# Turning the attention weights and the spread of scores by DMA instead of on TensorE

## The chip, the cores and the metric

The kernel runs on one core of a Trainium2 chip. Its engines work side by side, each through a queue of its own in order: TensorE (PE: matmuls and transposes, whose results go to PSUM banks), VectorE (DVE), ScalarE (ACT), GpSimd (POOL), and SyncE (SP), which only issues DMA transfers here. They wait for each other by semaphores. The metric is the device time of one execution, in microseconds (us); less is better.

## The reference, cut to what matters

There are 128 graphs of 128 nodes with 256 features in f32, and an adjacency of 0 and 1 for each graph (one in eight entries set). Two residual layers follow each other:

```python
# layer 0: a gated graph network, 3 steps with shared GRU weights
h = relu(layernorm(x))
for i in range(3):
    m    = h @ weight[i]
    aggr = A^T @ m                       # A = (adj != 0), for each graph
    h    = gru_cell(aggr, h, w_ih, w_hh, b_ih, b_hh)
x = x + h
# layer 1: graph attention
h  = relu(layernorm(x))
Wh = h @ W
s  = Wh.sum(-1)                          # one score for each node
e  = leaky_relu(s[:, :, None] + s[:, None, :], 0.2)
e  = where(adj == 0, -inf, e)
x  = x + softmax(e, -1) @ Wh
```

Two things in layer 1 concern the change. The score of the *second* node, s[q], has to stand along the free dimension of every partition p (the spread of scores). And the weights e[p, q] are needed with q on the partitions when they are multiplied with h, so they have to be transposed (128 x 128 for each graph).

## The kernel before, in words

**Tiling.** The graphs are worked in 32 groups of G = 4. "rows" tiles have nodes on partitions, 4 graphs x 256 features; "hT" tiles have features on partitions, two halves k of 4 x 128 nodes. All working tiles stay on chip; only x, the adjacency and the output move to and from HBM.

**One group.** `group` loads x and adj, normalises (`normed`), and goes through the three GRU steps. Each step sums over edges (`edge_sums`, line 596: f32 state split into three bf16 parts so that the product with a 0/1 matrix is exact) and multiplies state and edge sums with composed weights in `products`. That is one level of a seven-product (Strassen-Winograd) scheme for blocks of two by two: partial sums x, y and q stand in six PSUM banks with one buffer each (`x_rz`, `y_rz`, `q_rz`, and the same with `_n`), matmuls go on accumulating into y after ACT has copied a stage of it out (line 691, tiles `t_rz` and `t_n`; line 701 copies x into y), and DVE adds q to the copies (line 694). After y_rz come the matmuls of y_n, then the next product on y_rz, which needs the copy of y_rz done. Steps 0 and 1 end in `gru`, step 2 in `gru_rows`, which leaves the new x in the tile x1.

**State between layouts.** Where the state changes between rows and hT (groups 3 and on), `turned_halves` does it without PE: ACT copies the f32 data as two planes of 16-bit halves (line 535), SP issues a DMA transpose of them (line 545), ACT puts the halves together again (line 539), once for each k.

**Attention.** `attention(g, ...)` works on x1: `normed` into h1; s by a multiply with the summed weights w1_sum and an accumulated sum (line 867); the mask as 0 or -BIG into e (line 885); the spread of s by four PE transposes of a broadcast column into a "misc" bank (line 891); on DVE the add of that bank (897), the add of s[p] (898), leaky ReLU (900), row maximum (902) and its negation (904); exponentials on ACT (909, with a table load); row sums and reciprocals (911, 912); four PE transposes of e into a "misc" bank (917) and an ACT copy into eT (919); `weighted` multiplies h1 by eT (610) and ACT evicts uT (615); the product with W (930); the update of x1 (935) and the store (938). The last group's attention runs in two halves of two graphs. h1 and eT have one buffer, e, s, uT two, "misc" has two banks.

**The order.** Nothing is issued in the order in which the code calls it. Every piece of work goes into `Plan` by `op(engine, cost in ns, function, reads, writes, ...)`, and `Plan.run` simulates the five queues from these costs: on each engine it takes what can start first, and among those the one with the lowest rank. The rank is the due time less the planned cost of what still depends on the piece, with `MARGIN` taken off ahead of the fixed chain of product matmuls. The product matmuls keep a fixed order of 96 turns (group, step) of SLOT = 18150 planner ns each. The exponentials have to follow a marked copy of turn (g + 2, 1) and then go ahead of everything on ACT. `two=True` marks an operation that holds the SBUF port that DVE and POOL share, `LAG` is the planned time between engines, 4000 for SP (line 545 asks for 4500). The order so found is what the hardware queues get.

The attention of a group is due at the end of the turn of its last step plus three slots:

```python
plan.due = (phase(g, L - 1) + 3) * SLOT
gru_rows(L - 1, hT, hs, aT, gs, rows, x1)
for lo, hi in ((0, G),) if g < NG - 1 else ((G // 2, G), (0, G // 2)):
    attention(g, a, x1, h1, lo, hi)
```

Of the kernel before, what the change touches and what calls it, by code (L numbers as in the profile page):

```python
# [9 lines left out]
BF16 = mybir.dt.bfloat16  # L10
I32 = mybir.dt.int32
U16 = mybir.dt.uint16
AF = mybir.ActivationFunctionType
OP = mybir.AluOpType
AX = mybir.AxisListType

P = 128
G = 4
# [2 lines left out]
SETS = 4  # L21
EARLY = 3
SLOT = 18150
MARGIN = 5000
GATES = 18150
BIG = 3.0e38

# [9 lines left out]
class Plan:  # L37
# [14 lines left out]
    def buf(self, tag):  # L52
        n, kind = self.tags[tag]
        if kind == "free" or kind == "turn":
            b = Buf(tag, tag, None)
            if kind == "turn":
                self.waiting.setdefault(tag, []).append((self.phase, len(self.waiting.get(tag, ())), b))
            return b
        key = (tag, self.group % SETS if kind == "set" else 0)
        uses = self.last.setdefault(key, [])  # L60
        b = Buf(tag, key, uses[-n] if len(uses) >= n else None)
        b.slot = (key[1], len(uses) % n)
        uses.append(b)
        return b
# [146 lines left out]
def kernel(  # L211
# [21 lines left out]
    nc = tc.nc  # L233
    B, N, D = x.shape
    L = weight.shape[0]
    KD = D // P
    NG = B // G
# [5 lines left out]
    work = ctx.enter_context(tc.tile_pool(name="work", bufs=1))  # L243
# [5 lines left out]
        "at": (1, "all", work, [P, G, N]), "a": (6, "all", work, [P, G, N]),  # L249
        "hT": (1, "set", work, [P, KD, GN]), "rows": (3, "turn", work, [P, G, D]),  # L250
        "pl": (1, "turn", work, [P, 2, 3, GN]), "plT": (1, "turn", work, [P, 2, 3, GN]),
        "r1": (1, "turn", work, [P, G, D]), "p3": (1, "turn", work, [P, G, D]),
        "hs": (2, "turn", work, [P, 4, H]), "aT": (2, "turn", work, [P, KD, GN]),
        "gs": (2, "turn", work, [P, 4, H]),
# [21 lines left out]
        "w1": (1, "all", const, [P, KD, D]), "w1_out": (1, "all", const, [P, KD]),  # L276
        "w1_sum": (1, "all", const, [P, D]),
    }
    DTYPE = {"at": I32, "a": BF16, "pl": U16, "plT": U16, "p3": BF16}
    phys = {}  # L280

    def make(tag, n, kind, pool, shape):
# [7 lines left out]
    def ap(b):  # L290
        return phys[(b.tag,) + b.slot]

    plan = Plan({t: v[:2] for t, v in BUFS.items()})
    op, buf = plan.op, plan.buf
# [179 lines left out]
    def normed(src, dst, lo=0, hi=G):  # L474

        st, mv, rs, nm = buf("st"), buf("mv"), buf("rs"), buf("nm")
        part = slice(lo, hi)
        for b in range(lo, hi):
            op("DVE", 415, lambda b=b: nc.vector.bn_stats(ap(st)[:, b, :], ap(src)[:, b, :]),
               [(src, b, b + 1)], [(st, b, b + 1)])  # L480

        def aggr():
            for b in range(lo, hi):
                nc.vector.bn_aggr(ap(mv)[:, b, :], ap(st)[:, b, :])
        op("DVE", 160 * (hi - lo), aggr, [st], [mv])

        def rstd():
            nc.gpsimd.tensor_tensor(ap(rs)[:, part], ap(mv)[:, part, 1], eps[:, part], OP.add)
            nc.gpsimd.tensor_tensor(ap(rs)[:, part], ap(rs)[:, part], neghalf[:, part], OP.pow)
        op("POOL", 1300, rstd, [mv], [rs])  # L490
        op("DVE", 170, lambda: nc.vector.scalar_tensor_tensor(
            ap(nm)[:, part], ap(mv)[:, part, 0], -1.0, ap(rs)[:, part], op0=OP.mult, op1=OP.mult),
           [mv, rs], [nm])
        for b in range(lo, hi):
            op("ACT", 600, lambda b=b: nc.scalar.activation(
                ap(dst)[:, b, :], ap(src)[:, b, :], AF.Relu, bias=ap(nm)[:, b:b + 1],
                scale=ap(rs)[:, b:b + 1]), [(src, b, b + 1), rs, nm], [(dst, b, b + 1)])

    def flat(b):
        return ap(b).rearrange("p q n -> p (q n)")  # L500
# [26 lines left out]
    def turned_halves(src, rows, dst):  # L527

        pl, plT = buf("pl"), buf("plT")

        def planes(b, k):
            return ap(b)[:, k, 0:2].rearrange("p two (g m) -> p two g m", g=G)
        for k in range(KD):
            units = [src] if rows else [(src, 2 * k, 2 * k + 2)]
            op("ACT", 960, lambda k=k: nc.scalar.copy(
                planes(pl, k), halves_of(src, rows)[:, k]), units, [(pl, k, k + 1)])
            transpose(pl, plT, k, 2)
            units = [(dst, 2 * k, 2 * k + 2)] if rows else [dst]
            op("ACT", 960, lambda k=k: nc.scalar.copy(  # L539
                halves_of(dst, not rows)[:, k], planes(plT, k)),  # L540
               [(plT, k, k + 1)], units)

# [272 lines left out]
    def phase(g, layer):  # L815
        return turns.index((g, layer))

    def group(g):
        graphs = slice(g * G, (g + 1) * G)
        plan.phase = phase(g, 0)  # L820
        plan.due = (plan.phase - 1) * SLOT
        rows0, at, a, hT = buf("rows"), buf("at"), buf("a"), buf("hT")
        op("SP", 100, lambda: nc.sync.dma_start(ap(rows0), x[graphs].rearrange("b n d -> n b d")),
           [], [rows0])
        op("SP", 100, lambda: nc.sync.dma_start(ap(at), adj[graphs].rearrange("b n m -> n b m")),
           [], [at])
        op("DVE", 420, lambda: nc.vector.tensor_scalar(ap(a), ap(at), 0.0, None,
                                                       op0=OP.not_equal), [at], [a])
        plan.due = (phase(g, L - 1) + 2) * SLOT
        normed(rows0, rows0)  # L830
        for layer in range(L):
            plan.phase = phase(g, layer)
            if layer == 0:
                if g < EARLY:
                    rows_to_T(rows0, hT)
                else:
                    turned_halves(rows0, True, hT)
                parts = parts_of(rows0)
            elif layer < L - 1:
                parts = turned_parts(hT)  # L840
            else:
                rows, x1, h1 = buf("rows"), buf("x1"), buf("h1")
                turned_halves(hT, False, rows)
                parts = parts_of(rows)
                op("SP", 100, lambda: nc.sync.dma_start(
                    ap(x1), x[graphs].rearrange("b n d -> n b d")), [], [x1])
            hs, aT, gs = buf("hs"), buf("aT"), buf("gs")
            node_sums(hT, hs, "POOL", 1390, 940)
            edge_sums(parts, a, aT)
            node_sums(aT, gs, "DVE", 690, 440)  # L850
            plan.cursor = plan.phase * SLOT
            if layer < L - 1:
                gru(layer, hT, hs, aT, gs)
        plan.due = (phase(g, L - 1) + 3) * SLOT
        gru_rows(L - 1, hT, hs, aT, gs, rows, x1)
        for lo, hi in ((0, G),) if g < NG - 1 else ((G // 2, G), (0, G // 2)):
            attention(g, a, x1, h1, lo, hi)

    def attention(g, a, x1, h1, lo, hi):
# [19 lines left out]
        def es():  # L879
            return ap(e)[:, part]  # L880

        def small(t):
# [1 line left out]
        cost = 155 + 134 * n  # L884
        op("DVE", 150 + 66 * n, lambda: nc.vector.tensor_scalar(
            es(), ap(a)[:, part], 0.0, -BIG, op0=OP.is_equal, op1=OP.mult), [(a, lo, hi)], [e])
        s_all = buf("misc")

        def turn_s():
            for b in range(lo, hi):  # L890
                nc.tensor.transpose(flat(s_all)[:, b * N:(b + 1) * N],
                                    ap(s)[:, b:b + 1].to_broadcast([P, P]), ident)

        def spread():
            return flat(s_all)[:, lo * N:hi * N].rearrange("p (b n) -> p b n", n=N)
        op("PE", 110 * n, turn_s, [s], [s_all], [e])
        op("DVE", cost, lambda: nc.vector.tensor_tensor(es(), es(), spread(), OP.add), [s_all], [e])
        op("DVE", cost, lambda: nc.vector.tensor_tensor(es(), es(), wide(s), OP.add), [s], [e],
           two=True)
        op("DVE", cost, lambda: nc.vector.scalar_tensor_tensor(  # L900
# [6 lines left out]
        def exps():  # L907
            for b in range(lo, hi):
                nc.scalar.activation(ap(e)[:, b, :], ap(e)[:, b, :], AF.Exp, bias=ap(low)[:, b:b + 1])
        op("ACT", 2600 + 390 * n, exps, [low], [e], turn=(g + 2, 1, "rz"))  # L910
        op("DVE", cost, lambda: nc.vector.tensor_reduce(small(den), es(), AX.X, OP.add), [e], [den])
        op("DVE", 170, lambda: nc.vector.reciprocal(small(rden), small(den)), [den], [rden])
        p_e, eT, uT = buf("misc"), buf("eT"), buf("uT")

        def turn():
            for b in range(lo, hi):
                nc.tensor.transpose(flat(p_e)[:, b * N:(b + 1) * N], ap(e)[:, b, :], ident)
        op("PE", 110 * n, turn, [e], [p_e], [eT])
        op("ACT", 190 + 100 * n, lambda: nc.scalar.copy(
            ap(eT)[:, part].rearrange("p b n -> p (b n)"), flat(p_e)[:, lo * N:hi * N]),  # L920
           [p_e], [(eT, lo, hi)])

        weighted(h1, eT, uT, lo, hi)
        for m in range(lo, hi, 2):
# [13 lines left out]
        op("SP", 100, lambda: nc.sync.dma_start(  # L938
            out[g * G + lo:g * G + hi].rearrange("b n d -> n b d"), ap(x1)[:, part]),
           [(x1, lo, hi)], [])  # L940

    weights()
    for g in range(NG):
# [33 lines left out]
```

## Time and profile before

| | |
|---|---|
| median of 3 runs | 2150.49 us (2149.06 to 2151.18) |
| span of the profiled run | 2151.8 us |
| granted TensorE clock, mean | 0.994 |
| ACT copies of line 535, line 539 | 122 of 1046 and 1043 ns; 122 of 1338 ns |
| transposes on PE in the attention | 128 at line 891, 128 at line 917 |
| DMA queue of SP | 24.5% of 16 engines' span |

The page gives, in this order: busy time of each engine with its share of the span and its number of instructions; the same in tenths over 40 equal slices; the DMA queues; the chain of work that ended last, followed back from the last instruction; the costliest groups of instructions, each with its line, engine, operation, tiles written and read, count, busy time, mean time of one, and the idle time of its engine just before it with what ended it. PE is TensorE's matmul row and PEld its weight loads. The ends of matmul records are modelled and overlap with the next, so that the distance from start to start says what a matmul costs.

### The profile page before, as it was taken

Reading aid. Unit: us, or ns where it says so; the run is one execution under the profiler, and the core shown is the slowest. Engines: PE = TensorE matmul, PEld = TensorE weight load, DVE = VectorE, ACT = ScalarE, POOL = GpSimd, SP = SyncE. Lnnn points to the kernel's source line nnn. Section 1 sums busy time; section 2 is a strip of 40 time slices with the busy share of each in tenths; the row PEclk is TensorE's granted clock in tenths of the full one; section 3 lists DMA queues with packets and bytes.
Section 4 is the critical chain, followed back from the end, with each engine's and each line's share of the span. In section 5 each row is a group of like instructions: output and inputs, shape, how many; then the busy total and the mean of one; then the engine's idle time right before and its main releaser. Section 6 shows DMA issues by size and latency. Waiting matters only on the chain.

```text
span 2151.8 us, 34116 instructions
## 1 busy us (share of the span) xinstructions
PE 2124.3 (99%) x12670; PEld 1894.7 (88%) x12670; DVE 1693.9 (79%) x3297; ACT 1543.7 (72%) x2675; POOL 948.4 (44%) x889
## 2 busy tenths in 40 slices
PE   8999999999999999999999999999999999999997
PEld 7888888998889998888998899998899988898885
DVE  5778887887877778777787877878777787877776
ACT  5567877776777777767777777777777778676673
POOL 5645453344544435443445534445534345334331
PEclk9999999999999999999999999999999999999998
DMA  4222122222322222212122223223222213212110
GB/s 142 45 50 50 43 43 64 59 50 50 70 62 57 60 50 50 69 50 69 42 52 65 67 52 62 48 53 66 62 57 60 50 45 69 74 36 49 40 50 30
DMA packets 301750, 121.49 MB, mean 56 GB/s; under 512 B 232976, under 2 KB 301328, under 8 KB 301584
## 3 DMA queue, kind: packets, MB, share of 16 engines
q1 hardware_dynamic: 301584, 119.31, 24.5%
q8 instruction: 99, 1.62, 0.3%
q14 instruction: 67, 0.55, 0.1%
HBM read 45.36 MB, written 16.78 MB: 29 GB/s over the span
## 4 chain that ended last, share of the span: by engine, by line
PE 92%; DVE 5%; DMA 1%; ACT 1%; issue 1%; POOL 0%; DVEq 0%; ACTq 0%; POOLq 0%
PE y_rz L654 14%; PE q_rz L654 10%; PE x_rz L654 10%; PE y_rz L661 8%; PE y_n L654 7%; PE misc L596 6%; PE q_rz L661 5%; PE x_rz L661 5%; PE x_n L654 5%; PE q_n L654 5%; PE misc L930 5%; PE y_n L661 4%; PE x_n L661 3%; PE misc L610 3%; PE q_n L661 3%
## 5 line engine op out<-in xcount | busy, mean ns | idle before, releaser
L624 POOL TENSOR_TENSOR hs<-hT 128x512 f32<-128x512 f32 x96 | 128.8, 1342 | 326.3 <-PE y_n L661 275.9
L556 POOL TENSOR_TENSOR r<-rows 128x512 f32<-128x512 f32 x128 | 146.5, 1163 | 259.8 <-ACT rows L539 170.9
L691 ACT COPY t_rz<-y_rz 128x512 f32<-128x512 f32 x192 | 112.0, 583 | 191.9 <-PE y_rz L654 111.1
L654 PE MATMUL y_rz<-hs,s_hh 128*128 128x256 f32 x768 | 198.6, 381 | 0.2 <-ACT t_rz L691 0.2
L654 PE MATMUL y_rz<-gs,s_x 128*128 128x256 f32 x768 | 197.4, 380 | 0.0
L694 DVE TENSOR_TENSOR t_rz<-t_rz,q_rz 128x512 f32<-128x512 f32 x192 | 131.1, 683 | 70.0 <-ACT t_rz L691 36.5
L654 PEld LDWEIGHTS y_rz<-gs,s_x 128*128 128x128 f32 x768 | 146.4, 191 | 20.0
L654 PEld LDWEIGHTS y_rz<-hs,s_hh 128*128 128x128 f32 x768 | 144.3, 191 | 21.2 <-ACT t_rz L691 1.8
L628 POOL TENSOR_TENSOR hs<-hT,hs 128x256 f32<-128x256 f32 x96 | 75.0, 789 | 196.2 <-PE q_n L661 186.1
L559 POOL TENSOR_TENSOR p<-r 128x512 bf16<-128x512 f32 x128 | 155.5, 1233 | 0.3
L798 POOL TENSOR_TENSOR x<-x,u 128x512 f32<-128x512 f32 x64 | 84.8, 1341 | 157.9 <-DMA x<-in_x_dram 83.6
L691 ACT COPY t_n<-y_n 128x512 f32<-128x512 f32 x192 | 112.4, 585 | 52.3 <-PE y_n L654 20.7
L694 DVE TENSOR_TENSOR t_n<-t_n,q_n 128x512 f32<-128x512 f32 x192 | 131.1, 683 | 23.8 <-ACT t_n L691 9.1
L599 ACT COPY aT<-misc 128x512 f32<-128x512 f32 x192 | 111.7, 584 | 38.0 <-PE misc L596 30.3
L654 PE MATMUL x_rz<-aT,s_x 128*128 128x256 f32 x512 | 131.5, 379 | 0.0
L654 PE MATMUL x_rz<-hT,s_hh 128*128 128x256 f32 x512 | 131.5, 379 | 0.0
L576 POOL TENSOR_TENSOR d<-hT,pl 128x512 f32<-128x512 f32 x64 | 84.1, 1318 | 93.9 <-ACT pl L574 84.1
L930 PE MATMUL misc<-w,uT 128*128 128x256 f32 x512 | 122.8, 384 | 0.3 <-ACT uT L615 0.2
L755 ACT ACTIVATE u<-u,bias_i 128x512 f32<-128x512 f32 x128 | 92.1, 721 | 37.8 <-DVE u L746 37.5
L654 PE MATMUL y_n<-hs,s_hh 128*128 128x256 f32 x384 | 114.5, 380 | 0.3 <-ACT t_n L691 0.2
L654 PE MATMUL y_n<-gs,s_x 128*128 128x256 f32 x384 | 114.3, 379 | 0.0
L763 DVE TENSOR_TENSOR hT<-u,d 128x512 f32<-128x512 f32 x128 | 110.1, 862 | 3.5
(212 smaller groups left out, 6425.7 us busy)
## 6 DMA issues: line engine op xcount, KB each, us to landing
rows<-in_x_dram SPq DMA_DIRECT2D x32, 512.0 KB, 4.3
x<-in_x_dram SPq DMA_DIRECT2D x32, 512.0 KB, 3.9
out_dram<-x SPq DMA_DIRECT2D x31, 512.0 KB, 2.9
at<-in_adj_dram SPq DMA_DIRECT2D x32, 256.0 KB, 2.9
plT<-pl SPq DMA_TRANSPOSE x186, 3.3
rz<-in_L_gnn_w_ih_dram SPq DMA_DIRECT2D x1, 768.0 KB, 5.0
e<-in_L_gnn_weight_dram SPq DMA_DIRECT2D x3, 256.0 KB, 5.6
rz<-in_L_gnn_w_hh_dram SPq DMA_DIRECT2D x1, 768.0 KB, 7.9
```

The source lines that it names most:

```text
L556: op("POOL", 1106, lambda part=part: nc.gpsimd.tensor_tensor(ap(r1)[:, part], ap(rows)[:, part], top(rows)[:, part], OP.subtract), [(rows, ...
L559: op("POOL", 1050, lambda part=part: nc.gpsimd.tensor_tensor(ap(p3)[:, part], ap(r1)[:, part], top(r1)[:, part], OP.subtract), [(r1, n, n ...
L596: nc.tensor.matmul(flat(ps)[:, b * N:(b + 1) * N], part(i, b, k), ap(a)[:, b, :], start=(i == 0), stop=(i == 2))
L599: op("ACT", 590, lambda k=k, ps=ps: nc.scalar.copy(ap(dst)[:, k, :], flat(ps)), [ps], [(dst, 2 * k, 2 * k + 2)])
L624: op(eng, cost, lambda: sub(ap(w)[:, 0:2, :], blocks()[:, 1::2, :], blocks()[:, 0:2, :], OP.subtract), [t], [(w, 0, 2)], two=True)
L654: nc.tensor.matmul(ap(bank)[:, half, :], ap(w)[:, i - 1, q, :], source(t, sums), start=(first and c == 0 and m == 0), stop=False, skip_gro ...
L661: nc.tensor.matmul(ap(bank)[:, m, half * P:(half + len(chunk)) * P], source(t, sums)[:, m * N:(m + 1) * N], ap(w)[:, i - 1, q:q + len(chun ...
L691: op("ACT", 590, lambda: nc.scalar.copy(ap(t), ap(y)), [y], [t])
L694: op("DVE", 690, lambda: nc.vector.tensor_tensor(ap(t), ap(t), ap(q), OP.add), [q], [t])
L755: op("ACT", 723, lambda j=j, cols=cols: nc.scalar.activation(ap(u)[:, cols], ap(u)[:, cols], AF.Tanh, bias=ap(W["bias_i"])[:, 2 * KD + j:2 ...
L763: op("DVE", 690, lambda j=j, d=d, cols=cols: nc.vector.tensor_tensor(ap(hT)[:, j, :], ap(u)[:, cols], ap(d), OP.add), [(u, lo, hi), d], [( ...
L930: nc.tensor.matmul(ap(ps)[:, b, :], ap(uT)[:, k, (m + b) * N:(m + b + 1) * N], ap(w1)[:, k, :], start=(k == 0), stop=(k == KD - 1))
```

## The change

For groups 0 to 29 both transposes of the attention leave PE. A new helper, `turned_halves_of`, does what `turned_halves` does for the state: ACT copies 16-bit halves of the source into "pe" (two planes of 4 x 128), SP issues one DMA transpose into "peT", ACT puts the halves together in the destination. It is used twice for each group: from s, read with stride 0 as a broadcast, into a new tile s_all in SBUF, and from e into eT. The eviction at line 919 and two uses of the "misc" banks go with it. The last two groups keep the transposes on PE. pe, peT and s_all have one buffer each.

It is meant to take transposes off the engine that multiplies. Along with it, planner numbers change: MARGIN, the costs of Relu, of the halves' copies and of the exponentials are set to other values, and the attention of the last two groups gets the same due time, 96.5 slots (97 and 98 before).

```diff
-MARGIN = 5000
+MARGIN = 6000
...
+        "pe": (1, "all", work, [P, 2, G, N]), "peT": (1, "all", work, [P, 2, G, N]),
+        "s_all": (1, "all", work, [P, G, N]),
...
     def normed(src, dst, lo=0, hi=G):
-            op("ACT", 600, lambda b=b: nc.scalar.activation(
+            op("ACT", 520, lambda b=b: nc.scalar.activation(
...
     def turned_halves(src, rows, dst):
-            op("ACT", 960, lambda k=k: nc.scalar.copy(
+            op("ACT", 1045, lambda k=k: nc.scalar.copy(
                 planes(pl, k), halves_of(src, rows)[:, k]), units, [(pl, k, k + 1)])
             transpose(pl, plT, k, 2)
-            op("ACT", 960, lambda k=k: nc.scalar.copy(
+            op("ACT", 1340, lambda k=k: nc.scalar.copy(
...
-        plan.due = (phase(g, L - 1) + 3) * SLOT
+        plan.due = min(phase(g, L - 1) + 3, len(turns) + 0.5) * SLOT
...
-        s_all = buf("misc")
-        op("PE", 110 * n, turn_s, [s], [s_all], [e])
-        op("DVE", cost, lambda: nc.vector.tensor_tensor(es(), es(), spread(), OP.add), [s_all], [e])
+        if g < NG - 2:
+            s_all = buf("s_all")
+
+            def spread():
+                return ap(s_all)
+            turned_halves_of(lambda: ap(s).bitcast(U16).rearrange("p (g two) -> p two g", two=2)
+                             [:, :, :, None].to_broadcast([P, 2, G, N]), s, s_all)
+        else:
+            s_all = buf("misc")
...
+        op("DVE", cost, lambda: nc.vector.tensor_tensor(es(), es(), spread(), OP.add), [s_all], [e],
+           two=g < NG - 2)
...
-        op("ACT", 2600 + 390 * n, exps, [low], [e], turn=(g + 2, 1, "rz"))
+        op("ACT", 2570 * (g < NG - 1) + 320 * n, exps, [low], [e], turn=(g + 2, 1, "rz"))
...
-        p_e, eT, uT = buf("misc"), buf("eT"), buf("uT")
-        op("PE", 110 * n, turn, [e], [p_e], [eT])
-        op("ACT", 190 + 100 * n, lambda: nc.scalar.copy(
-            ap(eT)[:, part].rearrange("p b n -> p (b n)"), flat(p_e)[:, lo * N:hi * N]),
-           [p_e], [(eT, lo, hi)])
+        eT, uT = buf("eT"), buf("uT")
+        if g < NG - 2:
+            turned_halves_of(lambda: halves_of_weights(e), e, eT)
+        else:
+            p_e = buf("misc")
...
+    def halves_of_weights(t):
+        return ap(t).bitcast(U16).rearrange("p g (m two) -> p two g m", two=2)
+
+    def turned_halves_of(halves, src, dst):
+
+        pe, peT = buf("pe"), buf("peT")
+        op("ACT", 1045, lambda: nc.scalar.copy(ap(pe), halves()), [src], [pe])
+        op("SP", 100, lambda: nc.sync.dma_start_transpose(
+            ap(peT).rearrange("p two g q -> p (two g) q"),
+            ap(pe).rearrange("p two g m -> p (two g m)")), [pe], [peT])
+        op("ACT", 1340, lambda: nc.scalar.copy(halves_of_weights(dst), ap(peT)), [peT], [dst])
```

More of the change, by code (lines that the diff above doesn't have):

```diff
@@ L278 @@
     }
-    DTYPE = {"at": I32, "a": BF16, "pl": U16, "plT": U16, "p3": BF16}
+    DTYPE = {"at": I32, "a": BF16, "pl": U16, "plT": U16, "pe": U16, "peT": U16, "p3": BF16}
     phys = {}
@@ L886, in attention, with turn_s, spread @@
             es(), ap(a)[:, part], 0.0, -BIG, op0=OP.is_equal, op1=OP.mult), [(a, lo, hi)], [e])
-        s_all = buf("misc")
[L889 to L895, printed above, removed]
-        op("PE", 110 * n, turn_s, [s], [s_all], [e])
-        op("DVE", cost, lambda: nc.vector.tensor_tensor(es(), es(), spread(), OP.add), [s_all], [e])
+        if g < NG - 2:
[6 more added lines that the diff above has]
+            s_all = buf("misc")
+            def turn_s():
+                for b in range(lo, hi):
+                    nc.tensor.transpose(flat(s_all)[:, b * N:(b + 1) * N],
+                                        ap(s)[:, b:b + 1].to_broadcast([P, P]), ident)
+            def spread():
+                return flat(s_all)[:, lo * N:hi * N].rearrange("p (b n) -> p b n", n=N)
+            op("PE", 110 * n, turn_s, [s], [s_all], [e])
+        op("DVE", cost, lambda: nc.vector.tensor_tensor(es(), es(), spread(), OP.add), [s_all], [e],
+           two=g < NG - 2)
         op("DVE", cost, lambda: nc.vector.tensor_tensor(es(), es(), wide(s), OP.add), [s], [e],
@@ L909, in exps, with turn @@
                 nc.scalar.activation(ap(e)[:, b, :], ap(e)[:, b, :], AF.Exp, bias=ap(low)[:, b:b + 1])
-        op("ACT", 2600 + 390 * n, exps, [low], [e], turn=(g + 2, 1, "rz"))
+        op("ACT", 2570 * (g < NG - 1) + 320 * n, exps, [low], [e], turn=(g + 2, 1, "rz"))
         op("DVE", cost, lambda: nc.vector.tensor_reduce(small(den), es(), AX.X, OP.add), [e], [den])
         op("DVE", 170, lambda: nc.vector.reciprocal(small(rden), small(den)), [den], [rden])
-        p_e, eT, uT = buf("misc"), buf("eT"), buf("uT")
-        def turn():
-            for b in range(lo, hi):
-                nc.tensor.transpose(flat(p_e)[:, b * N:(b + 1) * N], ap(e)[:, b, :], ident)
-        op("PE", 110 * n, turn, [e], [p_e], [eT])
-        op("ACT", 190 + 100 * n, lambda: nc.scalar.copy(
-            ap(eT)[:, part].rearrange("p b n -> p (b n)"), flat(p_e)[:, lo * N:hi * N]),
-           [p_e], [(eT, lo, hi)])
+        eT, uT = buf("eT"), buf("uT")
[3 more added lines that the diff above has]
+            p_e = buf("misc")
+            def turn():
+                for b in range(lo, hi):
+                    nc.tensor.transpose(flat(p_e)[:, b * N:(b + 1) * N], ap(e)[:, b, :], ident)
+            op("PE", 110 * n, turn, [e], [p_e], [eT])
+            op("ACT", 190 + 100 * n, lambda: nc.scalar.copy(
+                ap(eT)[:, part].rearrange("p b n -> p (b n)"), flat(p_e)[:, lo * N:hi * N]),
+               [p_e], [(eT, lo, hi)])
         weighted(h1, eT, uT, lo, hi)
```

## The prediction

> **What bounds the kernel now.** I read the page first (busy shares, the 40 slices, the chain that ended last), then the groups of TensorE (PE) and ScalarE (ACT) by form, who waited for whom, the timeline of one period in the middle, and last the timeline of the end.
>
> ```profile
> PE 2124.3 (99%) x12670; PEld 1894.7 (88%) x12670; DVE 1693.9 (79%) x3297; ACT 1543.7 (72%) x2675; POOL 948.4 (44%) x889
> ...
> PE   8999999999999999999999999999999999999997
> ...
> PE 92%; DVE 5%; DMA 1%; ACT 1%; issue 1%; POOL 0%; DVEq 0%; ACTq 0%; POOLq 0%
> ```
>
> PE is busy in every slice, and 92% of the chain that ended last is PE work. The two groups that the change takes away, and the waits on which PE loses most, are these:
>
> ```profile
> L917 PE MATMUL misc<-ident,e 128*128 128x128 f32 x128 | 20.8, 284 | 6.0 <-ACT e L909 6.0
> L891 PE MATMUL misc<-ident,s 128*128 128x128 f32 x128 | 20.1, 275 | 2.1 <-DVE hw L867 1.5 <-DVE x L935 0.5
> ...
> PE misc L917 <- ACT e L909: 6.0, 2, 4.2
> PE q_rz L654 <- DVE gs L624: 3.4, 1, 3.4
> ```
>
> All PE waits on the list come to less than 25 us, so no buffer or transfer holds PE up in the middle: time goes only where PE instructions go. The "mean" of 275 to 284 ns is not what a transpose costs, because matmuls overlap. What one costs is read from starts in the timeline:
>
> ```profile
> 1504.63 0.61 PE L661 MATMUL y_n<-s_x,gs 128*128 128x128 f32 x4
> 1505.08 0.60 PE L891 MATMUL misc<-ident,s 128*128 128x128 f32 x4
> 1505.52 1.03 PE L661 MATMUL y_rz<-s_hh,hs 128*128 128x256 f32 x4
> ...
> 228.11 0.59 PE L654 MATMUL y_n<-gs,s_x 128*128 128x256 f32 x2
> 228.54 0.60 PE L917 MATMUL misc<-ident,e 128*128 128x128 f32 x4
> 228.97 1.03 PE L654 MATMUL y_rz<-hs,s_hh 128*128 128x256 f32 x4
> ```
>
> Four transposes of s hold PE from 1505.08 to 1505.52, 0.44 us; four of e from 228.54 to 228.97, 0.43 us.
>
> **What the Trainium skill says.** "Perfetto Trace Analysis", section "Identifying the Most-Contended Engine", says that a matmul's busy share is a bad measure of roofline because pipelined instructions look different in a trace; here the weight loads (88%) and the start-to-start times agree that PE is full, and the gap between 284 ns and 0.11 us per transpose shows the warning. "TensorE: Matmul & The Clock Gate", part "PE-mode transpose", gives some 275 ns for a transpose in a kernel's context; that is the record's length here (275 to 284), but queued among others one costs 0.11 us of PE, and the measurement decides. "DMA: Bandwidth & Descriptors", section "DMA Transpose (X-bar)", limits the DMA transpose to 2-byte elements, which is why f32 data goes as two 16-bit halves with a copy on each side; the trace shows that form already (lines 535, 545, 539). "SBUF — State Buffer", section "SBUF: two separate sides", says that a DVE operation with two SBUF inputs and a GpSimd operation that reads SBUF exclude each other for a whole instruction; the trace agrees: line 803 takes 684 ns in the median, and 1.55 us at 234.19, where POOL's line 798 had started at 233.93 and ran 1.26 us.
>
> **The change part by part.**
>
> *Removed from PE.* Groups 0 to 29 lose both sets of transposes: 30 x (0.44 + 0.43) = 26.1 us. In the middle PE has no idle time to swallow this, so it comes off the end, unless something new makes PE wait. Also gone: 30 evictions of line 919 (592 ns each, 17.8 us of ACT) and 60 of the uses of the two "misc" PSUM banks, which frees banks for edge sums and products.
>
> *Added on ACT.* Four copies of 1024 16-bit elements in each of 30 groups. The nearest rows are the same shape:
>
> ```profile
> L539 ACT COPY rows<-plT 128x1024 uint16<-128x1024 uint16 x64 | 82.2, 1338 | 0.0
> L535 ACT COPY pl<-hT 128x1024 uint16<-128x1024 uint16 x64 | 64.3, 1046 | 1.8 <-DVE hT L763 1.8
> ...
> plT<-pl SPq DMA_TRANSPOSE x186, 3.3
> ```
>
> That is 2 x 1.05 + 2 x 1.34 = 4.8 us for a group, less 0.6 for line 919: 4.2 us, or 125 us over 30 groups. The copy that spreads s reads one element many times (stride 0), which no row shows; from below it is the 1.05 us of a plain copy, from above the 1.34 us of the strided one; I take 1.05, and the difference is 9 us of ACT at most. In a period of three turns (1500.0 to 1563.7) ACT is busy 48.6 of 63.7 us; afterwards about 52.8 of 62.8, or 84%. ACT doesn't become the bound by load. By order it can: ACT runs its queue in order, and behind a 1.34 us copy may stand the eviction of y_rz (line 691). Without other PE work between, PE needs y_rz back 0.87 us after its last matmul (the y_n matmuls), and the eviction takes 0.59: some 0.25 us of slack. In the trace ACT stood idle before 150 of the 192 evictions of y_rz (111.1 + 80.6 us), so it has room; and the 122 pairs of such copies that it runs now cost PE nothing that the list of waits shows. I put 2 to 3 us on PE for all 120 new copies (some 0.02 us each).
>
> *Added transfers.* 60 DMA transposes of the size of line 545's two-plane ones: 3.3 us to landing in the median (3.0 to 5.4). The queue SP is in order, so what stands behind one is the next load, store or transpose; a transpose holds the queue 1.3 us to issue. The 16 engines are 24.5% busy; 60 more beside 186 of up to 1.5 times the size is some 3 to 5 points more. Hidden.
>
> *Longer chains in the attention.* s reaches the add (line 897) by copy 1.05, issue and landing 3.3, copy 1.34, about 6 us instead of 0.6. At 1504.1 s was complete, the add ran at 1505.7 and the exponentials (line 909) at 1512.0; the add would move to about 1510 and the exponentials to some 1517. The next step, line 917, ran only at 1546.5, and eT was read at 1561.3. The second chain, from e to eT, is again about 6 us. So 34 us of slack between the exponentials and the use of e's transpose takes both. The shared pair pe/peT is used for s up to about 1511 and for e from about 1518, so it doesn't block.
>
> *DVE.* Line 897 reads SBUF in place of PSUM: 0.69 us either way (line 898 is the SBUF row), plus at times a wait for POOL; DVE is at 79%, with the work off PE's path. Hidden.
>
> *Planner numbers and due times.* The new costs for Relu, halves and exponentials and the wider margin only reorder; I put nothing on them. The common due time (96.5 slots for groups 30 and 31 in place of 97 and 98) moves the last group's attention forward against the one before. It acts on the tail alone, where the chain of waits reads:
>
> ```profile
> 2117.66 0.61 DVE e L897
> 2118.29 0.70 DVE e L898
> 2119.01 0.70 DVE e L900
> 2119.74 0.70 DVE top L902
> ...
> 2136.67 0.69 ACT e L909 x2
> ...
> 2137.67 2.07 PE misc L610 x8
> ...
> 2140.21 3.78 PE misc L930 x8
> ...
> 2147.87 0.48 DVE x L935
> ```
>
> From 2115.6 to 2137.0 DVE is busy 19.95 of 21.4 us, from 2137.0 to the end 2.43 of 14.8. The score work of group 30 (2117.7 to 2120.4, 2.8 us, and its four updates of x at line 935, 1.6 us) stands ahead of group 31's. If it moves behind, the last exponentials come up to 4.4 us earlier; but group 30's own product then ends later, and may end last. Bounds: 4.4 us gained to about 3 us lost; I take 1 gained.
>
> *Sum.* 2150.5 - 26.1 + 2.5 - 1.0 = 2125.9, so 2126 us.
>
> **The rivals.**
>
> *A. The freed PE time stays freed: 2126 us.* For it: PE is full and nothing waits long. Against it: ACT is asked for 125 us more.
>
> *B. ACT's order gives about half back: 2139 us.* The transposes of s also stand where PE needs them: at 1505.08 they follow y_n and fill PE until y_rz is back. The eviction at 1504.45 took 0.59 us and ended at 1505.04, so without filler the next y_rz product is released with hardly anything to spare. If each of the 120 new copies delays an eviction by 0.1 us beyond its slack, or each of 60 lost fillers uncovers 0.2 us, 12 to 13 us return: 2126 + 13. Against it: ACT's idle time ahead of those evictions.
>
> *C. Nothing measurable: 2150 us.* It needs 24 us of new waits, 0.2 us for each new copy, or transposes that lay in gaps anyway. Only those of the last two groups do so, and those stay.
>
> *D. Slower: 2172 us.* [...]If each holds up an eviction by 0.4 us (half of the 1.2 us mean copy, less the 0.25 us slack), that is 120 x 0.4 = 48 us: 2126 + 48 = 2174, less 2 for what other PE work covers. A late landing would do the same, since ACT's queue would stand at the second copy with y_rz's eviction behind it: the longest landing was 5.4 us, and the planner allows 4 us for the new transposes against 4.5 for the old. Against it: the present copies of just this shape, twice as many, have cost no such waits: ACT waited for a landing once, for 0.2 us.
>
> *E. The tail gains its whole 4.4 us and more, and nothing is given back: 2119 us.* 2150.5 - 26.1 - 4.4 = 2120, less a microsecond of the waits of line 917 that go.
>
> **How the numbers follow.** A 0.60, B 0.18, C 0.04, D 0.11, E 0.07. A scatters some 5 us about its value for the tail and the copies. The range from 2116 to 2146 holds A, E and nearly all of B, and leaves out C and D (0.15) and a little of B. 0.2% is 4.3 us: faster is A, B and E, 0.85; same is C, 0.04; slower is D, 0.11.
>
> **What would show it.** PE's transposes of s and e fall from 128 each to 8 each, and PE's busy time falls by some 25 us while its share of the span stays at 98 or 99%. ACT's busy time rises by about 125 us to 1669. The DMA transposes number 246, at about 3.3 us to landing. The list of PE's waits stays under 40 us; if instead y_rz and y_n products wait for line 691 by tens of microseconds, B or D is right, and the second copy waiting for landings would point to the transfers. The last stretch without product matmuls stays near 36 us; if it grows by more than 4, the due times are to blame. The forecast is wrong if PE's share falls below 97%.

## The result and the profile after

The median is 2141.32 us (6 runs, 2139.5 to 2146.02) against 2150.78 us for the kernel before in the same comparison: ratio 0.9963, 95% interval 0.9951 to 0.9976. That is 9.5 us less, where 24.5 were forecast. The profiled run was one of the longer ones, with a span of 2144.0 us, 7.8 less than the profiled run before.

Of the page after, the row of busy times, TensorE's 40 slices, and two lines of DMA issues (KB each, median us to landing):

```profile
PE 2100.0 (98%) x12430; PEld 1869.2 (87%) x12430; DVE 1726.6 (81%) x3297; ACT 1638.7 (76%) x2765; POOL 963.1 (45%) x889
...
PE   8999999999999999999999999999999999999997
...
plT<-pl SPq DMA_TRANSPOSE x186, 3.7
peT<-pe SPq DMA_TRANSPOSE x60, 3.1
```

PE has 240 instructions and 24.3 us less, as it should. But the span shrank by a third of that. At this resolution nothing shows where the rest went: the row of PE's slices is the same, digit for digit. The same stretch of both kernels by windows shows it (length, then busy time and instructions of PE, PEld, DVE, ACT and POOL, granted clock, DMA share, GB/s). Before:

```profile
200.00:2000.00 1800.00, 1797.40 (x10858) 1613.32 (x10857) 1439.72 (x2809) 1330.77 (x2290) 800.66 (x745) 1.00 0.25 56
```

After:

```profile
200.00:2000.00 1800.00, 1784.68 (x10654) 1596.49 (x10653) 1485.74 (x2815) 1424.59 (x2386) 822.09 (x748) 1.00 0.30 64
```

PE idled 2.6 of 1800 us before and 15.3 after, at the same clock. VectorE (DVE) takes 46 us more here for practically the same instructions (2815 and 2809). The waits of PE after (us in total, times, longest us) name what it stood for:

```profile
PE y_rz L656 <- ACT t_rz L693: 10.0, 15, 1.8
PE misc L932 <- DVE x L950: 4.9, 2, 4.4
PE misc L612 <- ACT eT L967: 4.8, 2, 2.9
PE q_rz L656 <- DVE gs L626: 3.9, 1, 3.9
PE y_n L656 <- ACT t_n L693: 3.2, 3, 1.3
```

Before, the first line read

```profile
PE y_rz L654 <- ACT t_rz L691: 0.2, 1, 0.2
```

Now a product on y_rz waits 15 times for the eviction of y_rz (line 693 is the old 691). The third is the new path of e: 1.90 us at 358 us, and 2.90 us near the end.

Busy time overlaps, so I also took the distance between the starts of successive PE matmuls. The sum of all, each at the median of its kind (line and columns), fell from 2100.6 to 2074.2 us: 26.4. The excess over that median between 200 and 2000 us rose from 9.1 to 27.5: 18.4 given back. After 2050 us it rose by another 1.7 (21.9 to 23.6), before 200 us and from 2000 to 2050 it fell by 1.8: in all -26.4 + 18.4 + 1.7 - 1.8 = -8.1. The spans differ by 7.8, since 0.3 us more lie outside PE's first and last start.

What one such wait looks like, from the timeline after (start, duration, engine, line; in brackets the idle time before and what ended it):

```profile
1540.77 2.22 POOL L558 TENSOR_TENSOR r<-rows 128x512 f32<-128x512 f32 x2 [3.65 <-ACT rz L741]
1540.93 1.17 DVE L748 TENSOR_TENSOR u<-u,t_n 128x256 f32<-128x256 f32 x1
...
1542.02 1.52 DVE L805 TENSOR_TENSOR x<-x,d 128x512 f32<-128x512 f32 x1
...
1542.95 2.48 POOL L561 TENSOR_TENSOR p<-r 128x512 bf16<-128x512 f32 x2
...
1544.37 1.03 PE L656 MATMUL y_rz<-gs,s_x 128*128 128x256 f32 x4
...
1544.59 1.13 DVE L829 TENSOR_SCALAR a<-at 128x512 bf16<-128x512 int32 x1
...
1546.10 1.05 PE L612 MATMUL misc<-eT,h 128*128 128x128 f32 x8
...
1547.21 0.43 DVE L748 TENSOR_TENSOR u<-u,t_n 128x256 f32<-128x256 f32 x1
...
1547.67 0.72 ACT L757 ACTIVATE u<-u,bias_i 128x512 f32<-128x512 f32 x1 [2.10 <-DVE u L748]
1548.30 0.57 ACT L693 COPY t_rz<-y_rz 128x512 f32<-128x512 f32 x1
...
1548.92 1.13 PE L656 MATMUL y_rz<-hs,s_hh 128*128 128x256 f32 x4 [1.76 <-ACT t_rz L693]
```

The last matmuls on y_rz start at 1544.37 and end about 1545.4, so that its copy could run then. It runs at 1548.30, since ahead of it in ACT's queue stands the tanh of line 757, which waits 2.10 us for DVE. No copy of halves stands between: the last one ended at 1544.60, before y_rz was ready. And DVE, which works with hardly a gap from 1540.1 on, is late because three of its operations took 1.17, 1.52 and 1.13 us while GpSimd worked at lines 558 and 561; the shortest records of these three DVE lines are 0.41, 0.67 and 0.41. That is 2.3 us too much, about what ACT then waited.

### The profile page after: what moved, and what is told of

It is laid out like the page before. It is cut to its first block, busy times and chain, and to the rows that moved or that the text cites. A ratio compares the mean times of both kernels' runs of the same rounds, so it can differ in the third digit from the quotient of the medians.

```text
span 2144.0 us, 33915 instructions
## 1 busy us (share of the span) xinstructions
PE 2100.0 (98%) x12430; PEld 1869.2 (87%) x12430; DVE 1726.6 (81%) x3297; ACT 1638.7 (76%) x2765; POOL 963.1 (45%) x889
## 3 DMA queue, kind: packets, MB, share of 16 engines
q1 hardware_dynamic: 364944, 135.05, 28.6%
## 5 line engine op out<-in xcount | busy, mean ns | idle before, releaser
L626 POOL TENSOR_TENSOR hs<-hT 128x512 f32<-128x512 f32 x96 | 140.6, 1465 | 212.2 <-PE y_n L663 142.9
L583 POOL TENSOR_TENSOR pl<-d,pl 128x512 bf16<-128x512 f32 x64 | 78.7, 1232 | 209.1 <-ACT pl L581 195.9
L561 POOL TENSOR_TENSOR p<-r 128x512 bf16<-128x512 f32 x128 | 160.0, 1269 | 0.2
L800 POOL TENSOR_TENSOR x<-x,u 128x512 f32<-128x512 f32 x64 | 95.3, 1492 | 66.5 <-ACT u L796 65.3
```

The costliest lines, as they stand in the source:

```text
L561: op("POOL", 1050, lambda part=part: nc.gpsimd.tensor_tensor(ap(p3)[:, part], ap(r1)[:, part], top(r1)[:, part], OP.subtract), [(r1, n, n ...
L583: op("POOL", 1150, lambda k=k, r=r: nc.gpsimd.tensor_tensor(part(pl, k, 2), ap(r), part(pl, k, 1), OP.subtract), [r], [(pl, k, k + 1)])
L626: op(eng, cost, lambda: sub(ap(w)[:, 0:2, :], blocks()[:, 1::2, :], blocks()[:, 0:2, :], OP.subtract), [t], [(w, 0, 2)], two=True)
L800: op("POOL", 1290, lambda cols=cols, part=part: nc.gpsimd.tensor_tensor(part(x1), part(x1), ap(u)[:, cols], OP.add), [(u, lo, hi)], [(x1, ...
```

## The experiments

All ratios are to the kernel before, run beside each on the same chip (medians 2148.9 to 2150.4). The runs were made on several chips; differences between them are of medians, and the ratios give the same within 1.4 us. Three theories are tried:

- LOAD: the four copies for each group fill ACT, and whatever its order, evictions come late (rival B).
- ORDER: the time is lost where ACT's queue has a tanh ahead of an eviction, and the tanh waits for DVE.
- PORT: DVE is late there because GpSimd holds the SBUF port that both use.

### The parts of the change

**e1_dma_only**: both DMA transposes with the old planner numbers and due times.

```diff
-MARGIN = 6000
+MARGIN = 5000
 # and the costs of Relu, halves, exponentials (520, 1045, 1340, 2570 + 320 n)
 # back to 600, 960, 960, 2600 + 390 n, and the due time as before
```

> Both transposes by DMA, with MARGIN, planned costs and due times of before. After has 18 us more of waits between the product matmuls than before, and these ate most of the 26 us. Theory ORDER (ACT's queue holds the eviction of y_rz behind a tanh whose input DVE brings later than planned): another order, other waits; anything from 2125 to 2150, with PE busy at 2100. Rival LOAD (the waits come from the 4.2 us of copies that each group adds to ACT, whatever the order): the same 18 us of waits, so 2141 within 3. Rival NUMBERS (the new planner numbers made the bad order): the waits go back to those of before, 2126 within 4.

2165.61 us, ratio 1.0078 (1.0065 to 1.0090): slower than before. Waits of PE in this run:

```profile
PE y_rz L656 <- ACT t_rz L693: 20.0, 27, 2.5
PE y_n L656 <- ACT t_n L693: 9.8, 12, 1.3
```

The same kinds of wait as in the change, 29.8 us in place of 13.2. That is outside every range expected of this run: NUMBERS falls, since it is worse without the new numbers, and ORDER's range ended 15 us too low. The planner numbers are worth 24.3 us (2165.61 less 2141.32) once the DMA transposes are there.

**e2_numbers_only**: the kernel before with the new numbers and due times.

```diff
-MARGIN = 5000
+MARGIN = 6000
 # the new costs and due times; all transposes stay on PE
```

> PE transposes of before, with MARGIN, planned costs and due times of after. LOAD: nothing added to ACT, so 2150 within 4. NUMBERS: the new waits appear here as well, 2165 to 2170. ORDER: another order, 2145 to 2170, no number of its own; waits, if any, again with ACT idle ahead of the eviction.

2145.4 us, 0.9982 (0.9975 to 0.9988). Without DMA transposes the numbers are worth 4 us, not 24.

**e3_weights_only** and **e4_spread_only**: the change with one of the two transposes left on PE.

```diff
-        if g < NG - 2:      # ahead of the spread of s (e3), or of the transpose of e (e4)
+        if False:
```

> As after, but s is spread by PE transposes in all groups. Half of the PE time goes: 13 us. LOAD: half of the waits, 9 us, so 2146. ORDER: the waits aren't in proportion: 2137 if there are none, up to 2155.

> As after, but the weights are turned by PE in all groups. 13 us less on PE. LOAD: half of the waits, 2146. ORDER: not in proportion to the copies, 2137 to 2155, and e3 and e4 differ though both add 2.4 us of copies to each group or 1.8.

e3 gave 2138.64 us, 0.9955 (0.9942 to 0.9967); e4 gave 2133.45, 0.9929 (0.9916 to 0.9943). Each alone beats both together. Against e2, which has their planner numbers, the spread of s by DMA brings 12.0 of the 13.2 us that it takes off PE, the weights 6.8 of 12.9, and both together 4.1 of 26.1. e4 came out 3.5 us below the lowest expected. So the loss isn't a fixed price for each copy; the order that the plan found for the two together is what is left to explain it.

**e9_due_only**: the kernel before with the new due times alone.

```diff
-        plan.due = (phase(g, L - 1) + 3) * SLOT
+        plan.due = min(phase(g, L - 1) + 3, len(turns) + 0.5) * SLOT
```

> The kernel before with the common due time alone; PE transposes, MARGIN and costs of before. The prediction gave the due time 1 us, with bounds of 4.4 gained and 3 lost. If the tail's order matters as the bounds say: 2144 to 2149, and the change lies after 2100 us in the trace. If the 4 us that the planner numbers gained without any DMA transpose came from costs or MARGIN, this is 2149 within 1.5.

2148.36 us, 0.9998 (0.9989 to 1.0006): nothing.

### What the lost time is

**e5_swap**: the change, with one thing done to the order that the plan returns: a tanh (line 757) that stands on ACT directly ahead of evictions (line 693) goes behind them. Nothing else moves.

```diff
+        for k, i in enumerate(act):             # act: ACT's part of the order
+            if i not in self.tanh:
+                continue
+            j = k
+            while j + 1 < len(act) and act[j + 1] in self.evict:
+                j += 1
+            if j > k and all(place[u] > place[act[j]] for u in users[i]):
+                order.remove(i)
+                order.insert(order.index(act[j]) + 1, i)
```

> The changed kernel with its plan as it is; after planning, where a tanh of line 757 stands directly ahead of evictions of y (line 693) in ACT's queue, it is put behind them. No work, cost or buffer changes. In the changed kernel 12.4 us of PE's waits lie between the matmuls of line 612 and the next y_rz, with ACT standing idle at such a tanh. ORDER: those waits go, 2129 within 3, and the list of PE's waits shows y_rz behind line 693 with less than 2 us. LOAD: ACT does as much work, 2141.

2129.17 us, 0.9906 (0.9893 to 0.9919): 12.2 us less than the change, with the same instructions and the same copies. Its waits of PE begin

```profile
PE misc L946 <- DVE x L964: 4.9, 2, 4.4
PE misc L624 <- ACT eT L981: 4.8, 2, 2.9
PE y_n L668 <- ACT t_n L705: 2.7, 3, 1.3
```

(lines are 12 to 14 higher here); y_rz for t_rz is down from 10.0 to 1.1, and the excess between 200 and 2000 us from 27.5 to 16.4. LOAD falls for this part: ACT was busy 1634.9 us here and 1638.7 in the change.

**e7_thin_pool**: the change, where GpSimd's operations of lines 558, 561 and 800 work on 16 of 256 columns from group 6 on. It leaves out the low parts of the edge sums and part of an added state in the other columns. The order of all engines and the work on the others stay.

```diff
-                ap(r1)[:, part], ap(rows)[:, part], top(rows)[:, part], OP.subtract),
+                ap(r1)[:, part, :c], ap(rows)[:, part, :c], top(rows)[:, part, :c], OP.subtract),
 # c = 256 for groups 0 to 5, 16 for the others; lines 561 and 800 likewise
```

> The changed kernel in its own order, but from group 6 on GpSimd's operations of lines 558, 561 and 800 work on 16 of 256 columns (32 of 512 at line 800), so the low parts of the edge sums and the added state are left out there; order and waits stay. PORT (DVE comes later than planned because GpSimd, running ahead of its planned place, holds the shared port: line 803 took 1.8 and 1.6 us where 0.69 is usual): DVE is back on time, the waits for line 693 after group 6 go, 2127 within 4. If DVE is late for another reason: 2138 or more.

2123.62 us, 0.9879 (0.9866 to 0.9892), 17.7 us less than the change. Its row of busy times:

```profile
PE 2093.8 (99%) x12430; PEld 1868.0 (88%) x12430; DVE 1568.0 (74%) x3297; ACT 1645.1 (77%) x2765; POOL 679.7 (32%) x889
```

DVE's 3297 instructions are untouched and take 158.6 us less. The group of one of its operations, after (count, busy us, mean ns, idle before):

```profile
L803 DVE TENSOR_TENSOR d<-d,rz 128x512 f32<-128x512 f32 x64 | 71.9, 1126 | 0.7
```

and in e7:

```profile
L806 DVE TENSOR_TENSOR d<-d,rz 128x512 f32<-128x512 f32 x64 | 49.5, 776 | 0.7
```

The excess between 200 and 2000 us is 9.8 (9.1 before the change), so nearly all 18.4 us are back. Thin operations also give their results earlier, but that isn't it: DVE waited 5.0 us for GpSimd in the change and 5.3 here, ACT never, and PE only once, at the start. PORT holds. The Trainium skill, "SBUF — State Buffer", section "SBUF: two separate sides", says that whichever of the two starts first keeps the shared ports for a whole instruction while the other waits, for a DVE operation with two SBUF inputs against a GpSimd one that reads SBUF. Line 803 has two, and its 1126 against 776 ns agrees.

In the change the loss needs both conditions: e5 and e7 take away one each. A count from ACT's timeline between 200 and 2050 us shows tanh records directly ahead of an eviction of line 693, how many of these waited for DVE, and for how long:

| kernel | tanh ahead of eviction | of them waiting for DVE | us | PE idle, 200 to 2000 us |
|---|---|---|---|---|
| before | 27 | 1 | 0.3 | 2.6 |
| e2, numbers only | 51 | 1 | 1.7 | 4.1 |
| after | 34 | 22 | 40.5 | 15.3 |
| e5, tanh behind | 6 | 3 | 4.5 | 6.1 |
| e7, thin GpSimd | 34 | 2 | 3.4 | 3.0 |
| e1, old numbers | 31 | 22 | 19.5 | 27.9 |
| e4, spread only | 47 | 20 | 8.8 | 2.2 |

Before and in e2 such pairs are about as frequent or more, but DVE is in time for them. In the change it is late; e5 takes away the pairs, e7 the lateness. The size of PE's loss doesn't follow from the count: in e4 the 20 waits are short (0.4 us each) and cost nearly nothing, and in e1 half the waiting of the change goes with nearly twice its idle time, a part of it waits of y_n.

DVE's lateness as such isn't new. These are all waits of a tanh for DVE, before and after:

```profile
ACT u L755 <- DVE u L746: 37.5, 24, 3.1
ACT u L757 <- DVE u L748: 51.0, 29, 2.6
```

Before, all but three of them fell where no eviction stood directly behind. Nor does DVE's total tell: it was busy 1763.8 us in e2, which loses little, and 1726.6 in the change.

**e6_swap_dma_only**: e5's move on e1.

> The same swap on the kernel of e1 (both DMA transposes with the numbers of before, 2165.6), which waits 20 us in that place. ORDER: 2146 within 5. LOAD: 2165.

2143.28 us, 0.9976 (0.9966 to 0.9986): the move takes 22.3 us off e1. What remains is y_n waiting for t_n (10.4 us in 12 waits) and y_rz for t_rz (5.8 us in 4). The move doesn't touch the first kind: there the eviction into t_n itself waits for DVE (19.6 us in 18 waits of ACT).

**e10_dma_costs**: the change with the new costs, but the old MARGIN and due times.

```diff
-MARGIN = 6000
+MARGIN = 5000
-        plan.due = min(phase(g, L - 1) + 3, len(turns) + 0.5) * SLOT
+        plan.due = (phase(g, L - 1) + 3) * SLOT
```

> Both DMA transposes with the planned costs of after (Relu 520, halves 1045 and 1340, exponentials), but MARGIN 5000 and the due times of before. With all numbers of before it was 2165.6, with all of after 2141.3. If the 24 us between come from costs that now agree with the chip (two copies planned at 960 take 1338): 2141 to 2148. If MARGIN makes the difference: 2160 to 2166. ORDER alone allows anything between, since each is a new order.

2153.54 us, 1.0016 (1.0010 to 1.0023), so between e1 and the change, as neither the costs alone nor MARGIN alone had been expected to give: the costs bring about 12 of the 24 us, margin and due time the other 12. PE waits for t_rz as long as in e1:

```profile
PE y_rz L656 <- ACT t_rz L693: 21.8, 25, 2.6
```

Only the waits of y_n for t_n are nearly gone (0.7 us in place of 9.8). No single number explains the 24 us; which of margin and due time matters together with the DMA transposes wasn't tried.

### The end, and the best version

**e8_three_on_pe**: the change with group 29's transposes left on PE too.

```diff
-        if g < NG - 2:      # in both places, and in two= of the add
+        if g < NG - 3:
```

> As after, but group 29 keeps its transposes on PE as well. In the changed kernel PE waited 2.9 us at 2056.9 for group 29's eT and then ran two microseconds of matmuls at half speed. If that wait is the detour's latency near the end, 3 to 5 us go: 2137 within 2, and the waits in the middle stay. If order decides everything, the new order may move the middle by 10 us either way.

2132.62 us, 0.9929 (0.9917 to 0.9941): 8.7 us less than the change. What it removes near the end, from the timeline of PE in the change:

```profile
2056.34 0.61 PE L663 MATMUL x_n<-s_x,aT 128*128 128x128 f32 x4
2059.86 3.78 PE L612 MATMUL misc<-eT,h 128*128 128x128 f32 x16 [2.90 <-ACT eT L967]
2063.43 1.91 PE L663 MATMUL q_rz<-s_hh,hs 128*128 128x256 f32 x4
2065.14 1.38 PE L663 MATMUL q_rz<-s_x,gs 128*128 128x256 f32 x4
...
2098.93 1.95 PE L612 MATMUL misc<-eT,h 128*128 128x128 f32 x16
```

PE waits 2.90 us for group 29's eT, and then its matmuls run at half speed: 3.78 us for what takes 1.95 at 2098.93. The granted clock is 0.50 from 2059.0 to 2065.8. From start to start, 2059.86 to 2066.35 took 6.49 us for 16 matmuls of 128 columns and 8 of 256, which at full speed take 1.79 + 2 x 0.86 = 3.5. So the wait cost about 6 us in all in this execution. In e8 it is gone. But the middle, which I had expected to stay, has another order too, so the 8.7 us can't be put on the end alone (PE idles 11.0 us there, 15.3 in the change): there y_n waits where y_rz did,

```profile
PE y_n L656 <- ACT t_n L693: 10.8, 11, 2.0
```

and ACT's own waits in e8 say why, the eviction into t_n waiting for the reader of the last t_n:

```profile
ACT t_n L693 <- DVE u L787: 16.7, 17, 1.9
```

**e11_swap_three_2tn**: e5 and e8 together, and a second buffer for t2_n, one of the two tiles that the profile shows as t_n, so that this eviction needn't wait.

```diff
-        "t2_rz": (1, "free", work, [P, 2, H]), "t2_n": (1, "free", work, [P, 2, H]),
+        "t2_rz": (1, "free", work, [P, 2, H]), "t2_n": (2, "free", work, [P, 2, H]),
```

> A candidate: group 29 on PE as in e8, the swap of e5, and a second buffer for the copy t2_n, whose single buffer made the eviction of y_n wait for DVE's read of it (10.8 us of PE in e8, 11 times). If that wait goes: 2132.6 - 10.8 = 2122 within 3. If it moves to t3_n or to DVE: 2130 or more. LOAD, already out of step with e5, would give 2132.

2115.87 us (2115.38 to 2117.76), 0.9848 (0.9835 to 0.9861), the best of all. Its row of busy times, and its waits of PE for evictions:

```profile
PE 2092.6 (99%) x12438; PEld 1867.4 (88%) x12438; DVE 1707.0 (81%) x3297; ACT 1643.9 (78%) x2762; POOL 973.8 (46%) x889
```

```profile
PE y_rz L668 <- ACT t_rz L705: 1.4, 2, 0.8
```

PE idles 1.5 us from 200 to 2000, and the waits for t_n are gone. The time is 6 us below the 2122 expected. How the 16.8 us against e8 divide between the moved tanh and the buffer wasn't tried. ACT is as busy as in the change, so its load was not what cost the time. A second buffer for t_rz as well wasn't tried.

**e12_swap_2tn_pe**: e11 with all transposes of the attention back on PE.

```diff
-        if g < NG - 3:      # in both places
+        if False:
```

> The kernel of e11 with all transposes of the attention back on PE: the swap, the second t2_n and the planner numbers of after stay. It tells how much of e11's 33 us belongs to the DMA transposes. If they are worth what the prediction took off PE (29 groups here, 29 x 0.87 = 25 us): 2116 + 25 = 2141 within 4. If the swap and the buffer alone made the gain: below 2130.

2143.8 us, 0.9972 (0.9963 to 0.9981). Against e11 that is 27.9 us by the medians, and 26.7 by the two ratios, as the two ran on different chips. In e11, 29 groups are relieved, at 0.87 us each: 25.2. So with evictions in time the DMA transposes bring about all that they take off PE, though the two kernels also have different orders. And e12 is 1.6 us below e2: moved tanh and buffer do next to nothing as long as transposes stay on PE.

## Why the prediction was wrong

- **Removed from PE: right.** 26.1 us were forecast, 26.4 came off the sum of start-to-start times, and e11 against e12 agrees with the price of 0.44 and 0.43 us for a set.
- **Added on ACT: the copies were priced right, their effect on PE was not.** The change's new groups on ACT:

```profile
L967 ACT COPY eT<-peT 128x1024 uint16<-128x1024 uint16 x30 | 40.6, 1354 | 0.6 <-DMA peT<-pe 0.6
L967 ACT COPY s_all<-peT 128x1024 uint16<-128x1024 uint16 x30 | 40.5, 1351 | 1.2 <-DMA peT<-pe 1.2
L963 ACT COPY pe<-s 128x1024 uint16<-128x1024 uint16 x30 | 31.4, 1045 | 3.3 <-DVE hw L869 3.3
L963 ACT COPY pe<-e 128x1024 uint16<-128x1024 uint16 x30 | 31.3, 1042 | 0.0
```

  The copy with stride 0 takes 1045 ns, the lower end that I took. ACT's busy time rose by 95, not 125 us. The records do add up to 126 more (144 for the copies less 18 for line 919), but neighbouring records on ACT overlap, and the busy time counts the overlap once. **The step that failed is the sum's term for new waits of PE, "2 to 3 us on PE for all 120 new copies": 18.4 us came back between 200 and 2000 us, and not because copies held evictions up.** I asked only whether an eviction could stand behind a copy. It stood behind a tanh that waited for DVE: 12.2 us of the time go when the tanh moves (e5), and with DVE in time (e7) all but 0.7 of the 18.4 go, every copy still in place. The free time of ACT ahead of evictions, which I gave as the reason for a small term, says nothing of that: at 1547 us ACT stood idle for 2.10 us and held the eviction up at once.
- **DVE: "hidden" was wrong.** It is not the add of line 907 (690 ns) that cost, but that DVE's lateness reached PE through ACT. The stretched operations and 37.5 us of a tanh's waits for DVE were in the trace before, and I quoted one of those operations; I followed them no further than DVE's own load.
- **Planner numbers: "I put nothing on them" was wrong.** They are worth 4 us alone and 24 with the DMA transposes. Without them the change is slower than before (e1). By what places in the order they do this isn't shown.
- **Due time: 1 us gained was forecast.** Alone it gave nothing (e9), within an interval from 2.4 us gained to 1.3 lost, which holds the forecast.
- **Transfers: right.** 60 more transposes land in 3.1 us, the share of the DMA engines went from 24.5 to 28.6%, ACT waited 1.8 us in all for landings in front of these copies.
- **Longer chains: right but for two groups.** At 358 us the product waits 1.90 us for eT; for group 29 it waits 2.90 us, and the slow matmuls that follow double it. "Slack of 34 us" was read from one group at 1500 us, and taken for all.
- **The rivals.** B (2139) came nearest in size, but by luck, for neither of its reasons: the copies don't delay evictions by themselves (e5 and e11 keep them), and at the place shown lost filler isn't the cause either: eight matmuls of line 612 stand there at 1546.10, and PE waits all the same. D's picture, an ACT queue that stands at a waiting instruction with y_rz's eviction behind it, was right, but with another instruction at its head, and in 22 places, not 120.
- **The signs that I named couldn't tell.** PE's busy time fell by 24.3 us, its share stayed at 98%, and its waits came to 39.4 us (23.3 before), all as I had said for 2126. A percent of the span is 21 us, nearly the whole forecast.
- **What stays open:** why DVE is late at a tanh ahead of an eviction in the change and in time there in e2, with the same GpSimd work and no fewer such pairs. The new order shifts which GpSimd operation falls beside which DVE operation; no run held that fixed with the DMA transposes in place.

## What to carry to other kernels

Time taken off a full engine is kept if every instruction that releases its buffers is still in time: go through the in-order queue of the evicting engine and ask of each instruction ahead of an eviction not only how long it runs but what it waits for. Where an order is computed from costs, a change of the work and a change of the costs are one change: try them apart, and look at what the new order puts ahead of the evictions. A path that has slack in the middle is to be looked at again in the last groups, where less other work is left to fill the wait. And a sign that is to tell forecasts apart has to be finer than their difference.

## What the runs showed of the hardware

- Of DVE's 1726.6 us, 158.6 went away when three GpSimd operations were cut to a sixteenth of their columns. Even the conversion of the adjacency at line 829, with one input, takes 1129 ns at most and 408 at least, and its mean falls from 837 to 474 ns in e7.
- A single wait of PE of 2.90 us was followed by 6.5 us of matmuls that take 3.5 us at full speed. The granted clock is 0.50 for 6.83 us there; the kernel before shows 1.00 at that place (2050 to 2100 us). The same wait comes back in e1, e5, e6 and e7, each time with a stretch at 0.50 behind it, of 3.4 us in the first three and 6.8 in e7. The Trainium skill, "TensorE: Matmul & The Clock Gate", section "Why this matters for your kernels", warns of idle gaps of more than some 3 us; here less was enough. In all fourteen traces every wait of PE of 2.7 us or more was followed by such a stretch, and of seven waits between 2.0 and 2.6 us four were (as 2.09 us in e3) and three weren't (as 2.59 us in e10).
